# Layer 0 and layer 3 of an adjacency GNN on one Trainium2 core: edge scores by maximum and minimum over sorted columns, and neighbour sums made in the first stage

## The chip, the core and the metric

The kernel runs on one core of one Trainium2 chip. A core has a matrix engine (TensorE, PE in the profile), a vector engine (VectorE, DVE), an activation engine (ScalarE, ACT), GpSimd (POOL) and SyncE (SP). Each works through its own instruction queue in order, and an instruction that waits holds everything behind it in its queue. SP, ACT and POOL also issue DMA transfers from their queues; 16 DMA engines carry them. The metric is the device time of one launch in microseconds; the kernel before takes 3124.82 us, the median of three runs (3122.06 to 3131.15).

## The reference, cut to what matters

```python
# x: (32, 512, 256) f32; adj: (512, 512) f32, symmetric pattern, 4386 non-zero entries
def gnn(h, A, W1, b1, W2, b2, Wa, ba, Wm, bm, beta1, beta2, beta3):      # layers 0 and 3
    pre_u = einsum('bud,dk->buk', h, W1[:256])
    pre_v = einsum('bvd,dk->bvk', h, W1[256:])
    hidden = relu(pre_u[:, :, None, :] + pre_v[:, None, :, :] + b1)
    S = sigmoid(einsum('buvk,ko->buvo', hidden, W2)[..., 0] + b2[0])
    a = einsum('buv,bud->bvd', S * A, h)
    m = einsum('uv,bud->bvd', A, h) * h
    return beta1 * h + beta2 * (a @ Wa + ba) + beta3 * (m @ Wm + bm)
x = gnn(x, adj, L0)                        # layer 0
x = x + relu((adj @ x) @ W.T + b)          # layer 1
f = x @ W1_2.T; f1 = f @ W2_2 + b2_2       # layer 2
c = softmax(leaky_relu(f1[i] + f1[j]) + adj)
x = c @ f + bias2 + x
return gnn(x, adj, L3)                     # layer 3
```

S is needed only where the adjacency has an entry, so it is computed per edge: for an edge (u, v) one takes row u of pre_u + b1, row v of pre_v, and needs the sum over 256 columns k of W2[k] * relu(pu[k] + pv[k]).

## The kernel before, in words

**Two paths.** A short prelude (`Counts`) counts entries per row of the adjacency and writes a number `excess`; if it is positive a dense path runs, else the sparse path. With the given inputs the sparse path runs, and only it is described.

**Groups.** The 32 batches are worked in 8 groups of 4 (`NB`). For each group and each of layers 0 and 3 there is a `Group` with a table in DRAM (1024 rows of 4 x 256 values: for every node its pre_u + b1 row and its pre_v row, for the four batches side by side), a matrix of scores in DRAM (`cells`, two halves), and small tiles on chip (`s`, `self_s`).

**Edges as items.** `Edges.build` turns the adjacency into 36 items of 128 edges each: 8 for every chunk of 128 nodes (`OWN`), of which partition p holds the first to eighth neighbour of node p, and 4 panels for the nodes with more neighbours. To do this it computes ranks, writes four `lists` to DRAM, and for the panels gathers four rows `got` of these lists by index (L368), each needing `inode`, computed last (L345 to L362). Entries on the diagonal are not items.

**The five kinds of streams** of a group, all Python generators:

- `first`: loads h, turns it over on PE (L556), stores hT to DRAM (`xT`, L768), and in `pre` multiplies by W1 (L570, L572). From each PSUM result `pre` makes `puv` on DVE and ACT (L574, L575), the score of the diagonal in two more DVE operations (L577, L578), and writes `puv` to the table on SP's queue (L582).
- `edges`: for each item, fetch the other end's rows from the table by index on POOL's queue (L607) into one of 5 buffers, some items ahead; the own end's rows (`mine`) once per chunk on SP's queue (L647). DVE adds the two, 128x1024 (L686). Then relu, times W2, and the sum over 256 columns for each batch: for every second item in one DVE operation of 128x1024 (L694) and four ACT accumulations (L672), for the others in four accumulating DVE operations of 128x256 (L702). Scores are finished every four items (exp on ACT, L592; L596, L597, L636 on DVE) and scattered into `cells` by index on POOL's queue (L601). Two calls, the very first and the very last, have `spare` buffers, a longer lead, and send every item by L694 and ACT.
- `middle`: loads the score matrix SA (L727, on POOL's queue), and per batch runs layer 0's rest, layers 1 and 2, and `pre` of layer 3. Layer 0's rest needs hWa and the neighbour sums mhT (`mhT`, PE L45 `adj,h` and DVE L750), made at the start of each batch, then zT (L848 on DVE), on which the next PE step L861 waits.
- `last`: layer 3's rest (hWa, mhT, L1001, L1010), out to DRAM. In the last group it is split into `last_before` and `last_behind`.
- `setup` streams: `Edges.build`, scaled weights, and zeroing of `cells` (L538, on SP's queue).

The call for group 0 is special: its hWa and mhT are made ahead (`middle_before`).

**What sets the order.** `sparse_path` gives each piece of each stream a due time in units of a group, and `weave` emits pieces by due time; pieces of kind "fill" (`first`, `last`) are held back and put where the middle stage says that it has room. `behind` adds order constraints that keep edge work behind the middle stage. A tile framework then adds semaphores and orders each engine's queue. PE's queue is thus fixed at build time.

Of the kernel before, what the change touches and what calls it, by code (L numbers as in the profile page):

```python
# [36 lines left out]
SPARE = NC // 2 * OWN * P + LINES  # L37
GROUP = NB * D
HELD = 8
# [8 lines left out]
class Model:  # L48


    def __init__(self, ctx, tc, a):
        nc = self.nc = tc.nc
        self.tc, self.a = tc, a
        const = self.const = ctx.enter_context(tc.tile_pool(name="const", bufs=1))
        self.ident = const.tile([P, P], F32, name="ident")
        make_identity(nc, self.ident)
        self.adj = const.tile([P, NC, N], F32, name="adj")
        for c in range(NC):
            nc.sync.dma_start(self.adj[:, c, :], a["adj"][c * P : (c + 1) * P, :])
        self.g0, self.g3 = self.gnn_first("L0_gnn"), self.gnn_first("L3_gnn")  # L60
# [36 lines left out]
    def gnn_first(self, L):  # L97
# [3 lines left out]
        w["b1bc"] = self.bcast(f"{L}_b1", D)  # L101
        w["W2bc"] = const.tile([P, D], F32, name=f"{L}_W2bc")
        nc.scalar.dma_start(w["W2bc"], a[f"{L}_W2"].rearrange("k o -> (k o)").partition_broadcast(P))
# [7 lines left out]
        return w  # L111

# [63 lines left out]
class Counts:  # L176
# [3 lines left out]
    def __init__(self, ctx, m):  # L180
# [4 lines left out]
        with tc.tile_pool(name="c_sb", bufs=2) as sb, tc.tile_pool(name="c_ps", bufs=1, space=PSUM) as ps:  # L185
# [17 lines left out]
            pc = ps.tile([1, NC], F32, name="pc")  # L203
            nc.tensor.matmul(pc, ones[:, 0:1], self.lines, start=True, stop=True)
            half = sb.tile([1, 2], F32, name="half")
            nc.vector.tensor_reduce(half, pc.rearrange("p (h c) -> p h c", h=2), AX.X, ALU.add)
            most = sb.tile([1, 1], F32, name="most")
            nc.vector.tensor_reduce(most, half, AX.X, ALU.max)
            nc.vector.tensor_scalar(self.excess, most, float(-LINES), None, ALU.add)
# [10 lines left out]
class Edges:  # L220
# [3 lines left out]
    def __init__(self, m, pool):  # L224
# [4 lines left out]
        self.value = pool.tile([P, ITEMS], F32, name="value")  # L229
        self.inode = pool.tile([P, 2 * PANELS], I32, name="inode")  # L230

        order = [item_of(0, j) for j in range(OWN // 2)]
        for lead, other in ((0, 2), (2, 1), (1, 3)):
            for j in range(OWN // 2):
                order += [item_of(lead, OWN // 2 + j), item_of(other, j)]
# [6 lines left out]
    def value_of(self, j):  # L242
        k = self.order.index(j)
        return self.value[:, k : k + 1]

# [3 lines left out]
    def build(self, counts, adjT, lists, psum, big, tmp):  # L249
# [66 lines left out]
        for c in (0, 2, 1, 3):  # L316
            at = slice(c, c + 1)
# [24 lines left out]
            self.slots(js, v, there, t, row[:, at], spare)  # L342
            yield

        js = slice(NC * OWN, ITEMS)  # L345
        pu = psum()[:, 0 : 2 * PANELS]
        ones_bf = bf2[:, 1024:1025]
        nc.vector.memset(ones_bf, 1.0)
        for k in range(2 * PANELS):
            h, q = divmod(k, PANELS)  # L350
            mm(nc, pu[:, k : k + 1], [(full[:, h * 2 + c, q * P : (q + 1) * P], ones_bf) for c in range(2)])
        u, node, slot, start, sp, v, there, t = (sheet(2 * PANELS) for _ in range(8))
        nc.vector.tensor_scalar(u, pu, float(HALF - 1), None, ALU.min)
        nc.vector.tensor_copy(node, u)
        nc.vector.tensor_scalar(node[:, PANELS:], u[:, PANELS:], float(HALF), None, ALU.add)
        inode = self.inode
        nc.vector.tensor_copy(inode, node)
        nc.vector.tensor_scalar(self.iu, node, 2.0, None, ALU.mult)
        nc.gpsimd.iota(slot, [[0, 2], [P, PANELS]], 0, 1, allow_small_or_imprecise_dtypes=True)
        nc.vector.tensor_scalar(start, u, float(N), None, ALU.mult)  # L360
        nc.vector.tensor_scalar(sp, slot, float(CELLS + NC // 2 * OWN * P), None, ALU.add)
        nc.vector.tensor_scalar(t, slot, 1.0, None, ALU.add)  # L362
        yield
        gots = []
        for k in range(2 * PANELS):
            gots.append(tmp.tile([P, 2 * N], F32, name=f"got{k}", tag=("h1", "hT1", "mhT0", "hWa0")[k]))
            index = bass.IndirectOffsetOnAxis(ap=inode[:, k : k + 1], axis=0)
            nc.gpsimd.indirect_dma_start(out=gots[k], out_offset=None, in_=lists, in_offset=index)  # L368
        yield
        for k in range(2 * PANELS):  # L370
# [4 lines left out]
                junk, rank, t[:, at], adj, ALU.is_equal, ALU.mult, accum_out=self.value_of(NC * OWN + k)  # L375
            )
            nc.vector.scalar_tensor_tensor(junk, rank, slot[:, at], ones, ALU.is_le, ALU.mult, accum_out=v[:, at])
            yield
        self.slots(js, v, there, t, start, sp, 0)
# [19 lines left out]
class Group:  # L399

    def __init__(self, sp, w, name):
# [3 lines left out]
        self.s = sp.grp.tile([P, ITEMS, NB], F32, name=f"s{name[0]}")  # L407
        self.self_s = sp.grp.tile([P, NC, NB], F32, name=f"self_s{name[0]}")
# [6 lines left out]
class Sparse:  # L415
# [3 lines left out]
    def __init__(self, ctx, m, counts, xr, outr, B):  # L419
# [12 lines left out]
        self.xT, self.x2T = (self.dram.tile([B, P, DC, N], F32, name=n) for n in ("xT", "x2T"))  # L432
        self.e = Edges(m, pool("edges", 1))
# [76 lines left out]
    def setup(self):  # L510
# [6 lines left out]

        edges = self.built = self.e.build(self.counts, self.adjT, self.lists, self.psum, self.big, self.act)
# [11 lines left out]
    def zeros_behind(self):  # L530
        self.zeros(self.cells["3"])
        yield

    def zeros(self, cells):
        for c in cells:
            flat = c[0:CELLS, :].rearrange("(q p a) b -> q p (a b)", q=4, p=P)
            for q in range(4):
                self.nc.sync.dma_start(flat[q], self.zero)  # L538
# [5 lines left out]
    def setup_rest(self):  # L544
        yield from self.rest
# [14 lines left out]
    def pre(self, g, b, hT):  # L560
# [3 lines left out]
        for c in range(NC):  # L564
# [9 lines left out]
            nc.vector.tensor_tensor(puv[:, 0, :], pp[:, 0:D], w["b1bc"], ALU.add)  # L574
# [788 lines left out]
```

## Time and profile before

| what | value |
|---|---|
| median of three runs | 3124.82 us |
| profiled execution, its own time | 3102.14 us |
| its span, first to last instruction | 3100.4 us |
| mean granted TensorE clock in it | 0.941 |
| PE busy | 2714.6 us (88%) |
| DVE busy | 2302.8 us (74%) |
| POOL busy | 1522.5 us (49%) |
| ACT busy | 1337.8 us (43%) |
| DMA bytes, mean rate | 679.40 MB, 219 GB/s |

How to read what follows: a group line names source line, engine, operation, tile written and tile read, shapes, a count, then busy time and mean duration of one; after the second bar comes the idle time of the engine just before these instructions and what ended it. A line of a waits view says which instruction waited for which, the total, how often, and the longest. A windows line gives a stretch in us from the span's start, its length, the busy time of each engine in it, the granted clock, the busy share of the DMA engines and the rate. fp32 matrix products appear as two passes each, and the counts are of passes.

### The profile page before, as it was taken

How to read it: one execution, taken by the hardware profiler on the slowest of the kernel's cores; microseconds unless marked ns; L12 is line 12 of the kernel's file. 1: busy time of each engine (PE TensorE's matmuls, PEld its weight loads, DVE VectorE, ACT ScalarE, POOL GpSimd, SP SyncE). 2: the span in 40 equal slices, each digit the busy share in tenths (PEclk: the TensorE clock that was granted, in tenths of full speed). 3: DMA queues.
4: the chain of work that ended last, by engine and by line, in shares of the span. 5: the costliest groups of instructions: out<-in, count | busy, mean ns of one | idle time of the engine just before them, and what ended most of it. 6: DMA issues, size and time to landing. Idle time of an engine off the chain costs nothing.

```text
span 3100.4 us, 32465 instructions
## 1 busy us (share of the span) xinstructions
PE 2714.6 (88%) x8645; PEld 1642.5 (53%) x8646; DVE 2302.8 (74%) x6026; ACT 1337.8 (43%) x4101; POOL 1522.5 (49%) x1312
## 2 busy tenths in 40 slices
PE   6366888889998999989998999989999899889957
PEld 3133444446654565546664565545664566545636
DVE  6783886889589875989589885888679795772761
ACT  3453554445345433545354442545335343453440
POOL 1462453556346563556346562565436563450561
PEclk9688988999999999999999999999999999999978
DMA  8874556786677766786668766787568766551753
GB/s 285 282 236 152 180 174 225 237 268 213 223 224 263 235 210 219 247 282 213 227 213 258 238 197 213 242 267 237 188 216 268 251 221 208 178 174 58 234 195 115
DMA packets 302719, 679.40 MB, mean 219 GB/s; under 512 B 52672, under 2 KB 170944, under 8 KB 294336
## 3 DMA queue, kind: packets, MB, share of 16 engines
q0 software_dynamic: 120384, 406.01, 41.0%
q1 hardware_dynamic: 163184, 234.01, 22.5%
q10 hardware_dynamic: 18960, 37.24, 3.2%
q8 instruction: 70, 1.15, 0.2%
q14 instruction: 121, 0.99, 0.1%
HBM read 531.12 MB, written 146.01 MB: 218 GB/s over the span
## 4 chain that ended last, share of the span: by engine, by line
PE 51%; DVE 18%; DMA 17%; issue 6%; ACT 4%; POOL 3%; SPq 0%; POOLq 0%; ACTq 0%; DVEq 0%
PE pst L45 24%; PE pst L1001 7%; DVE rows L686 6%; DMA table<-puv 5%; DMA rows<-table,iv 5%; PE pst L570 3%; DVE rows L702 3%; PE pst L861 3%; PE pst L1010 3%; PE pst L572 3%; DMA cells<-s,cell 3%; DVE rows L694 3%; PE pst L883 2%; PE pst L840 2%; DMA SA<-cells 2%
## 5 line engine op out<-in xcount | busy, mean ns | idle before, releaser
L601 POOL DMA_INDIRECT cells<-s,cell x576 | 691.1, 1200 | 740.7 <-DMA cells<-s,cell 370.3
L607 POOL DMA_INDIRECT rows<-table,iv x554 | 663.3, 1197 | 672.7 <-DMA table<-puv 148.1
L686 DVE TENSOR_TENSOR rows<-rows,mine 128x1024 f32<-128x1024 f32 x554 | 670.8, 1219 | 164.7 <-DMA rows<-table,iv 148.8
L672 ACT ACTIVATE rows<-rows 128x256 f32<-128x256 f32 x1096 | 442.9, 407 | 516.7 <-DVE rows L694 511.1
L45 PE MATMUL pst<-adj,h 128*128 128x512 f32 x1024 | 451.3, 592 | 0.3 <-PE pst L941 0.3
L702 DVE SCALAR_TENSOR_TENSOR rows<-rows,L_gnn_W2bc 128x256 f32<-128x256 f32 x1120 | 415.9, 419 | 1.8
L45 PE MATMUL pst<-L_gnn_Wa,hT 128*128 128x256 f32 x1024 | 264.3, 410 | 118.6 <-DMA hT<-xT 64.6
L694 DVE SCALAR_TENSOR_TENSOR rows<-rows,L_gnn_W2bc 128x1024 f32<-128x1024 f32 x274 | 332.3, 1216 | 0.3
L45 PEld LDWEIGHTS pst<-adj,h 128*128 128x128 f32 x1024 | 192.8, 190 | 222.4 <-issue 218.4
L45 PEld LDWEIGHTS pst<-L_gnn_Wa,hT 128*128 128x128 f32 x1024 | 207.7, 208 | 165.8 <-issue 53.1
L45 PE MATMUL pst<-eT,feats 128*128 128x512 f32 x512 | 231.5, 606 | 12.4 <-ACT eT L953 12.4
L45 PE MATMUL pst<-adjT,zW 128*128 128x512 f32 x512 | 227.8, 597 | 6.2 <-ACT zW L865 6.2
L1001 PEld LDWEIGHTS pst<-hWa,SA 128*128 128x128 f32 x896 | 213.7, 328 | 7.7 <-issue 4.5
L1001 PE MATMUL pst<-hWa,SA 128*128 128x256 f32 x896 | 216.8, 398 | 0.0
L861 PE MATMUL pst<-WT,hT 128*128 128x256 f32 x512 | 150.3, 459 | 75.9 <-DVE hT L848 75.9
L672 ACT ACTIVATION_READ_ACCUMULATOR rows<-rows 128x1 f32 x1096 | 206.7, 189 | 0.0
L809 ACT COPY flat<-SA 128x512 f32<-128x512 f32 x128 | 137.6, 1128 | 155.0 <-PE pst L45 60.1
L840 PE MATMUL pst<-flat,hWa 128*128 128x512 f32 x448 | 196.8, 592 | 0.0
L861 PEld LDWEIGHTS pst<-WT,hT 128*128 128x128 f32 x512 | 118.0, 235 | 114.9 <-DVE hT L848 88.1
L575 ACT COPY puv<-pst 128x256 f32<-128x256 f32 x256 | 93.7, 370 | 183.8 <-DVE puv L574 168.1
L574 DVE TENSOR_TENSOR puv<-pst,bc_L_gnn_b 128x256 f32<-128x256 f32 x256 | 105.0, 416 | 90.3 <-DMA table<-puv 53.8
L45 PEld LDWEIGHTS pst<-eT,feats 128*128 128x128 f32 x512 | 97.5, 193 | 127.5 <-issue 109.8
(170 smaller groups left out, 3979.3 us busy)
## 6 DMA issues: line engine op xcount, KB each, us to landing
table<-puv SPq DMA_DIRECT2D x256, 256.0 KB, 5.5
SA<-cells POOLq DMA_DIRECT2D x64, 1024.0 KB, 7.0
h<-in_x_dram SPq DMA_DIRECT2D x64, 512.0 KB, 6.4
mine<-table SPq DMA_DIRECT2D x64, 512.0 KB, 5.3
hT<-xT SPq DMA_DIRECT2D x36, 512.0 KB, 5.1
h<-x2s SPq DMA_DIRECT2D x36, 512.0 KB, 4.1
xT<-hT ACTq DMA_DIRECT2D x32, 512.0 KB, 5.5
x2T<-yT SPq DMA_DIRECT2D x32, 512.0 KB, 5.3
```

Of the source, the lines that this page charges most:

```text
L45: nc.tensor.matmul(out, lhsT, rhs, start=(n == 0), stop=(n == len(pairs) - 1))
L574: nc.vector.tensor_tensor(puv[:, 0, :], pp[:, 0:D], w["b1bc"], ALU.add)
L601: self.nc.gpsimd.indirect_dma_start(out=g.cells[half], out_offset=bass.IndirectOffsetOnAxis(ap=at, axis=0), in_=s, in_offset=None)
L607: self.nc.gpsimd.indirect_dma_start(out=rows, out_offset=None, in_=g.table, in_offset=bass.IndirectOffsetOnAxis(ap=at, axis=0))
L672: self.behind(nc.scalar.activation(part, part, AF.Identity, accum_out=g.s[:, k, b : b + 1]))
L686: self.behind(nc.vector.tensor_tensor(rows, rows, other, ALU.add))
L694: nc.vector.scalar_tensor_tensor(by_entry, by_entry, 0.0, w2, ALU.max, ALU.mult)
L702: nc.vector.scalar_tensor_tensor(part, part, 0.0, w["W2bc"], ALU.max, ALU.mult, accum_out=at)
L809: self.nc.scalar.copy(flat[:, r, :], SA[r][:, :, b])
L840: nc.tensor.matmul(pz, hWa[:, r, cs], flat[:, r, :], start=(r == 0), stop=False)
L861: nc.tensor.matmul(pw[:, at], zT[:, d, cs], m.WT_1[:, d, :], start=(d + k == 0), stop=(d * k == 1))
L1001: nc.tensor.matmul(pz[:, k * D : (k + 1) * D], SA[r][:, cs, b], hWa[:, r, :], start=(r + k == 0), stop=False)
```

## The change

**Sorted columns.** The columns of W1 are permuted so that columns with positive W2 stand first, scaled by -W2 or W2, and the score of an edge becomes a sum over columns of a maximum (positive W2) or a minimum (negative W2) of two table rows, less a number per node (`less`) that is added up while `puv` is made. In a band of 32 columns around the middle (`MIXED`), where the sign can differ between inputs, a multiplication by `sign` turns one into the other. `sorted` does the permutation at run time with small matrix products, once per layer. An item now takes three DVE operations, of 4x144, 4x32 and 4x112 columns, in place of the addition, and then either four ACT accumulations or one DVE reduction; the multiplication by W2 is gone. ACT takes every second item (two of three in the calls with `spare`).

**Diagonal as turns.** The four chunks of diagonal entries become four more turns of the edge loop (40, `TURNS`), with rows fetched on SP's queue and scores stored on SP's queue; `pre` makes no diagonal score any more. The `less` numbers go through DRAM (16 stores on SP) and 4 small gathers per call on POOL's queue for the panels.

**Neighbour sums with the first layer.** For groups 1 to 7 mhT of layer 0 is made in `first` from the h that is loaded there, stored to DRAM (`mhTs`, SP) and loaded in `middle`, which no longer loads h. `first` of group 2 moves from due time 0.67..0.93 to 0.1..0.45.

**Lists sooner, zeros later.** The gathers of `got` stand before the items of the third chunk. Zeroing moves to POOL's queue; that of layer 3's `cells` waits behind the middle stage.

```diff
+TURNS = ITEMS + NC
+MIXED = slice(D // 2 - 16, D // 2 + 16)
+    def sorted(self, w, t, psum):
...
+        mm(nc, pr[:, 0:1], [(before, positive[:, 0:1])])
+        mm(nc, pr[:, 1:2], [(before, positive[:, 1:2]), (ones, positive[:, 0:1])])
+        mm(nc, pr[:, 2:3], [(ones, positive[:, c : c + 1]) for c in range(DC)])
...
+            nc.vector.tensor_scalar(place[:, c, :], row, to[:, c : c + 1], None, ALU.is_equal)
...
+                nc.tensor.transpose(pt[:, r * P : (r + 1) * P], w["W1"][:, r, c * P : (c + 1) * P], self.ident)
+            nc.scalar.copy(W1T[:, c, :], pt)
...
+        nc.vector.tensor_copy(vs, pw[:, 0:D])
...
+            nc.vector.tensor_tensor(w["W1"][:, r : r + 2, :], by_two(ps), by, ALU.mult)
...
# Counts
+            nc.vector.tensor_scalar(positive, m.cols[:, :, 0, :, 0], 0.0, None, ALU.is_gt)
...
# Edges
+        order = [item_of(0, j) for j in range(OWN // 2)] + [ITEMS]
...
+            order.append(ITEMS + other)
...
# setup
+        self.m.sorted(self.m.g0, self.big(F32, 2048), self.psum)
     def zeros_behind(self):
+        self.behind(self.nc.vector.memset(self.zero, 0.0))
         self.zeros(self.cells["3"])
...
-                self.nc.sync.dma_start(flat[q], self.zero)
+                self.nc.gpsimd.dma_start(flat[q], self.zero)
     def setup_rest(self):
+        self.m.sorted(self.m.g3, self.big(F32, 2048), self.psum)
# pre
-            nc.vector.tensor_tensor(puv[:, 0, :], pp[:, 0:D], w["b1bc"], ALU.add)
+            nc.vector.scalar_tensor_tensor(
+                puv[:, 0, :], pp[:, 0:D], 1.0, w["bu"], ALU.mult, ALU.add, accum_out=part
+            )
             nc.scalar.copy(puv[:, 1, :], pp[:, D:])
-            both = self.small.tile([P, D], F32, name="both", bufs=1)
-            nc.vector.tensor_tensor(both, pp[:, D:], puv[:, 0, :], ALU.add)
             nc.vector.scalar_tensor_tensor(
-                both, both, 0.0, w["W2bc"], ALU.max, ALU.mult, accum_out=g.self_s[:, c, b : b + 1]
+                junk, puv[:, 0, MIXED], 1.0, w["sign"][:, 0, :], ALU.mult, ALU.mult, accum_out=mixed
             )
# edges
+        def less(ks):
...
+                self.behind(nc.vector.tensor_tensor(s, s, by, ALU.subtract))
...
+                    nc.sync.dma_start(diagonal, g.s[:, k, :])
...
-            self.fetch(rows, g, e.iv[:, j : j + 1])
+            if j < ITEMS:
+                self.fetch(rows, g, e.iv[:, j : j + 1])
+            else:
+                nc.sync.dma_start(rows, places[c, 1])
...
-            self.behind(nc.vector.tensor_tensor(rows, rows, other, ALU.add))
+            self.behind(nc.vector.tensor_tensor(rows[:, :, first], rows[:, :, first], other[:, :, first], ALU.max))
+            nc.vector.tensor_tensor(rows[:, :, mixed], rows[:, :, mixed], sign, ALU.mult)
+            self.behind(nc.vector.tensor_tensor(rows[:, :, behind], rows[:, :, behind], other[:, :, behind], ALU.min))
...
+            if k == TURNS // 2:
+                for q in range(2 * PANELS):
+                    nc.gpsimd.indirect_dma_start(
+                        out=g.less[:, NC + q, :], out_offset=None, in_=g.less_dram, in_offset=index
+                    )
...
-            if spare or k % 2 == 1 and k < ITEMS - 3:
-                nc.vector.scalar_tensor_tensor(by_entry, by_entry, 0.0, w2, ALU.max, ALU.mult)
+            if k % 3 < 2 if spare else k % 2 == 1 and k < TURNS - 3:
                 summed.append(lambda k=k, rows=rows: sums(k, rows))
...
-                for b in range(NB):
-                    nc.vector.scalar_tensor_tensor(part, part, 0.0, w["W2bc"], ALU.max, ALU.mult, accum_out=at)
+                nc.vector.tensor_reduce(g.s[:, k, :], rows, AX.X, ALU.add)
# first
+            if i > 0:
+                for mhT in self.mhT(h, hT, 3):
+                    yield
+                self.nc.sync.dma_start(self.mhTs[i + b], mhT)
             yield from self.pre(g, b, hT)
# fresh, middle_one
-            h = self.act.tile([P, NC, D], F32, name="h1")
-            self.nc.sync.dma_start(h, self.xr[i])
+            mhT = self.act.tile([P, DC, N], F32, name="mhT1", tag="h1")
+            self.nc.sync.dma_start(mhT, self.mhTs[i])
...
-        else:
-            for mhT in self.mhT(h, hT, 0):
-                yield
# sparse_path
-            first = spread(FIRST, start - 0.86, start - 0.6)
+            first = spread(FIRST, 0.1, 0.45) if t == 2 else spread(FIRST, start - 0.86, start - 0.6)
...
-            (sp.edges(g0, ("yT", "mhT3") if t == 0 else ()), edges0, ""),
+            (sp.edges(g0, ("yT", "mhT0", "hWa0") if t == 0 else ()), edges0, ""),
```

## The prediction

> **What bounds the kernel now.** I read the windows first, cut at the points where groups change, since a mean hides stages (columns: stretch; its length; busy PE, PEld, DVE, ACT, POOL; granted clock; DMA share; GB/s).
>
> ```profile
> 0.00:85.00 85.00, 57.30 (x177) 30.99 (x178) 58.15 (x212) 33.86 (x87) 16.35 (x29) 0.92 0.84 288
> 85.00:262.00 177.00, 81.09 (x218) 44.49 (x218) 117.88 (x227) 80.56 (x341) 102.30 (x86) 0.75 0.74 256
> 262.00:474.00 212.00, 170.48 (x491) 91.78 (x492) 150.67 (x402) 103.35 (x276) 85.97 (x76) 0.87 0.48 151
> 474.00:711.00 237.00, 206.52 (x610) 112.13 (x609) 191.16 (x526) 106.85 (x324) 123.71 (x106) 0.94 0.77 250
> 711.00:1059.00 348.00, 329.60 (x1074) 200.29 (x1073) 281.79 (x764) 155.26 (x464) 187.29 (x160) 0.98 0.72 236
> 1411.00:1763.00 352.00, 332.40 (x1071) 201.60 (x1069) 281.89 (x764) 155.65 (x464) 187.07 (x162) 0.97 0.73 235
> 2479.00:2880.00 401.00, 376.50 (x1229) 230.50 (x1228) 259.84 (x687) 164.97 (x439) 159.30 (x137) 0.97 0.51 166
> 2880.00:3028.00 148.00, 102.83 (x342) 72.86 (x340) 104.67 (x138) 69.78 (x313) 93.47 (x73) 0.86 0.67 222
> ```
>
> Five like periods, 711 to 2479, take 348 to 359 us each with PE busy 330 to 335 (95%), DVE 282 (80%). PE bounds them; their idle PE sums to 107 us. Before them PE is idle 41.5 + 30.5 us (262 to 711), after them 24.5: 203.7 us in 262 to 2880. The first 262 us (one group's first edges) and the 148 from 2880 (the last edges) are bound by the edge chain.
>
> Next, what PE waits for between 262 and 2880, and what DVE waits for in 85 to 262 and over the whole span (columns: total, times, longest):
>
> ```profile
> PE pst L861 <- DVE hT L848: 75.9, 21, 8.5
> PE pst L952 <- DVE cols L912: 37.6, 6, 8.7
> PE pst L952 <- DVE ex L913: 30.6, 21, 3.3
> ...
> DVE big L374 <- DMA got<-lists,inode: 16.0, 1, 16.0
> ...
> DVE puv L574 <- DMA table<-puv: 53.8, 24, 4.5
> ```
>
> The first three, 144 of PE's 204, are middle-stage results that stand on DVE behind edge work. The fourth is a hole in the opening stage, the fifth counts under the rivals. Last, the groups that the change edits (count, busy, mean ns):
>
> ```profile
> L686 DVE TENSOR_TENSOR rows<-rows,mine 128x1024 f32<-128x1024 f32 x554 | 670.8, 1219 | 164.7 <-DMA rows<-table,iv 148.8 <-DMA mine<-table,iu 13.2 <-issue 1.7
> L672 ACT ACTIVATE rows<-rows 128x256 f32<-128x256 f32 x1096 | 442.9, 407 | 516.7 <-DVE rows L694 511.1 <-ACT x L943 3.2 <-ACT puv L575 1.1
> L702 DVE SCALAR_TENSOR_TENSOR rows<-rows,L_gnn_W2bc 128x256 f32<-128x256 f32 x1120 | 415.9, 419 | 1.8
> L694 DVE SCALAR_TENSOR_TENSOR rows<-rows,L_gnn_W2bc 128x1024 f32<-128x1024 f32 x274 | 332.3, 1216 | 0.3
> ```
>
> The timeline of DVE gives the pitch, since neighbours overlap by about .084 us: two additions take 2.36, a 1024-column operation 1.135, a 256-column accumulating one about .345 (starts at 929.51 and 929.85).
>
> ```profile
> 927.24 2.36 DVE L686 TENSOR_TENSOR rows<-rows,mine 128x1024 f32<-128x1024 f32 x2
> 929.51 0.42 DVE L702 SCALAR_TENSOR_TENSOR rows<-rows,L_gnn_W2bc 128x256 f32<-128x256 f32 x1
> ```
>
> **DVE per item.** Before: an item for ACT costs 2 x 1.135 = 2.27 us, an item for DVE 1.135 + 4 x .345 = 2.515. After: the additions of 1024 (1.219), 512 (.684) and 256 columns (.419) lie on .149 + 1.045 ns per column, which gives .751 for the maximum (576), .283 for the multiplication (128), .617 for the minimum (448): 1.651 less 3 x .084 = 1.40. A DVE turn adds one reduction of 128x1024. None is in the trace; bounds are .75 (a third below an elementwise pass, faster than any f32 row here of two inputs) and 2.0 (four accumulating passes of 256 with their reads, .419 + .081 each). I take an elementwise pass, 1.135, since it reads the same columns: 2.535 a turn.
>
> An ordinary call then goes from 16 x 2.27 + 20 x 2.515 = 86.6 to 18 x 1.40 + 22 x 2.535 = 81.0, and with its few score operations (.6 before; subtractions of `less` bring about 2.3) from 87.2 to 83.3: -3.9. `pre` loses two 256-column operations a chunk and gains one of 32 with its read, 1.015 to .455 us, 16 chunks a call: -9.0. Two calls a period: -26 of 282 (9%). A `spare` call goes from 36 x 2.27 = 81.7 to 27 x 1.40 + 13 x 2.535 less overlaps, about 73. Whole kernel: DVE 2303 to about 2100.
>
> The Trainium skill, VectorE: DVE Perf Modes, section Rules for kernel authors, speaks against this part: operation count is what to minimize, and three replace one here. In the rows four 256-column operations cost 1.38 where one of 1024 costs 1.135, .08 for each added one, so the count matters little at this size. By the rule with no overlap a turn would be 1.65, +160 us of DVE over 640 turns, and two thirds of the DVE gain would go.
>
> **ACT, POOL, DMA, SP.** ACT accumulates .407 + .189 a piece, 2.38 a turn: +4.8 us an ordinary call (ACT is at 44%, hidden). POOL: 4 gathers of `less` a call at 1.2 + .3 issue, +6 on about 94; hidden at 53%. DMA: own-end rows 33.6 MB and mhTs stores 14.7 MB against 679, +7%, share .72 to about .77; hidden unless it delays `table` writes. SP gains 64 row fetches, 32 more diagonal stores, 28 mhTs stores and 16 `less` stores, about 140 entries, each able to wait; what stands behind them is the `puv` store (L582), whose lateness DVE pays at L574. I cost them at nothing: SP's entries are waiting for their producers anyway; uncovered they are rival C.
>
> **PE.** mhT of a group is 4 x 16 passes of 512 columns at .4295 (16 in 6.87 us), 27.5 us. Groups 2 to 7 only move it to `first`: total unchanged. Group 1's goes into the first 262 us, where PE is busy 138 of 262: -27.5 in the span after, full gain if that idle takes it (bounds -27.5, 0 if its products hold up `pre`, whose rows the edges want). Sorting adds 7 us of PE per layer; layer 0's is ahead of all, layer 3's lies within edges of group 0: 0 each beyond the term below.
>
> **Opening, 0 to 262: -12 (bounds -35, +15).** The 16.0 us hole goes, as `got` is asked for some turns ahead. About 16 list scans of .67 us (+10.7) now stand ahead of the first row addition, not after. Layer 3's zeros, 4.2 MB, leave a stretch with DMA at .84 and 288 GB/s: 15 us of transfers, half taken as exposed, -8. `spare` DVE work falls by 8.5 but the chain is mostly latency: -4. The sorting chain stands ahead of the first W1 product; the first table write came only at 38.1 us, behind the zeros, so I count +5 of its estimated 17. Sum -12. Here the Trainium skill (DMA: Bandwidth & Descriptors, section Issuing engines are not separate DMA queues) says that another issuing engine saves only issue time; by it the zeros of layer 0 give nothing, and only the delay of layer 3's would, some -8.
>
> **Idle PE in 262 to 2880: -92 of 203.7 (bounds 0, -204).** In 262 to 711 there are 72 us idle, because there is no filler: `first` of group 2, due at 0.67, now comes from 0.1 and carries 31.7 + 27.5 = 59 us of PE. I take half, 35: the rest is chains within one batch (softmax), and group 1's edges must still be scheduled with DVE. In the five periods, 107 us: the queue on DVE ahead of L848, L912 and L913 shrinks; DVE goes from 80% to 73%, or with a period of 338 to 76%. Waiting behind a backlog falls faster than load; 40% gives 43, 8.6 a period, 353 to about 344. What is late next is PE itself, whose floor is 329.5. In 2479 to 2880, 14 of 24.5, as mhT of the last group no longer stands at the head of its batches. mhT in `middle` is now a load, issued early on SP; if it comes late, PE waits at L847 in place of running it.
>
> **Tail, 2880 to the end: +3 (bounds -8, +15).** Four more turns of latency-bound edges at about 4 us an item, two thirds covered by the cheaper ones, and `less` gathers on POOL, which there is busy 93 of 148.
>
> **Sum**, against the profiled execution, 3102.1: -27.5 - 12 - 35 - 43 - 14 + 3 = -128.5, so 2974. The median of the runs stands at 3124.82 / 3102.14 = 1.0073 of it: 2995.
>
> **Rivals.** A: as forecast, 2995 (own range 2930 to 3050). B: waits are latency in the chains, not DVE load, and only the moved mhT, the opening and the tail count: -36.5, 3066 profiled, 3088. For it: 21 waits at L861 are near 3.6 us each, three DVE operations deep, and shorter operations shorten them little; against it: L686 operations of 2.36 stand directly ahead of them. C, slower: the SP queue holds up the `puv` stores. Each hit costs DVE and then PE 2.24 us (53.8/24). With 140 new entries the gain of 128.5 is gone from .92 us an entry; half of them at 2.24 would be 157, net +28, 3153. For it: SP already stands 484.7 us in front of `puv` stores. Against: these waits are for producers, and only 24 of 256 were felt. D: the reduction costs far more than 2.0; DVE becomes the bound at 344 us a period: 256 + 44 x (t - 1.135) = 344 at t = 3.1 us. At 2.0, DVE is 294, above 282: no gain from backlog, B. E: nearly all the idle goes, mhT and sorted load together, -190: 2912 profiled, 2933. F: the change does not do what it says, if excess were positive and the dense path ran; the trace shows sparse items in all groups, and the test stays, so under .01.
>
> **Chances.** A .55, B .17, C .11 (incl. a larger opening loss), D .03 (half slower), E .13, F .01. Range 2910 to 3095: E, A and B inside, C and D out. Faster than before by over 0.3% (about what a measurement can tell here): A, B, E and half of D, .87; slower .11; same .02.
>
> **What would show it.** DVE busy near 2100; groups of 640 at .75, .28 and .62 us, 334 reductions at 1.2; `adj,h` products before 262; no wait on `got`; L848's wait under half of 75.9; periods of 338 to 346. Wrong: a reduction near 2, a grown wait at L574 for the table, or an opening over 265 us.

## The result and the profile after

The changed kernel takes 3208.57 us (median of four runs) against 3125.64 for the kernel before: a ratio of 1.0263, 95% interval 1.0238 to 1.0288. It is slower by 2.6%, where 2995 was forecast. The profiled execution has a span of 3212.1 us, 111.7 more than before's 3100.4. The medians differ by only 82.9 us: before's profiled execution (3102.14) lies 0.7% under its median and the changed kernel's (3213.80) 0.2% above, so differences read off the two profiles are some 29 us too large in all.

The page's line of busy times of the changed kernel:

```profile
PE 2753.3 (86%) x8729; PEld 1667.2 (52%) x8730; DVE 2109.8 (66%) x5600; ACT 1337.7 (42%) x4185; POOL 1482.3 (46%) x1406
```

Its groups by form, for the work that was priced (count, busy and mean ns; behind the second bar the idle time before, and what ended it):

```profile
L815 DVE TENSOR_TENSOR rows<-rows,mine 128x576 f32<-128x576 f32 x610 | 458.2, 751 | 356.6 <-DMA rows<-table,iv 348.9 <-issue 7.7
L833 DVE TENSOR_REDUCE s<-rows 128x4 f32<-128x1024 f32 x324 | 392.3, 1211 | 2.8
L817 DVE TENSOR_TENSOR rows<-rows,mine 128x448 f32<-128x448 f32 x610 | 375.8, 616 | 0.0
L816 DVE TENSOR_TENSOR rows<-rows,L_gnn_sign 128x128 f32<-128x128 f32 x610 | 169.4, 278 | 0.0
```

Every price of an instruction was right to within 2%: .751, .278, .616 and 1.211 us against .751, .283, .617 and 1.219 forecast, DVE 2109.8 against "about 2100". DVE lost 193 us of work, and the profiled execution became 112 us longer. What grew is in the first line of the groups: the maximum waited 356.6 us for its rows, where before's addition waited 164.7.

The windows of the changed kernel, cut where the zT addition of a group's first batch starts (columns as in the prediction):

```profile
0.00:279.00 279.00, 181.87 (x559) 102.55 (x561) 164.00 (x580) 104.92 (x363) 124.08 (x146) 0.88 0.77 257
279.00:543.00 264.00, 239.29 (x707) 125.73 (x705) 162.11 (x452) 120.61 (x326) 90.95 (x92) 0.95 0.64 209
543.00:887.00 344.00, 270.73 (x840) 167.33 (x840) 240.41 (x594) 149.28 (x470) 178.04 (x164) 0.89 0.68 220
887.00:1259.00 372.00, 338.31 (x1072) 204.69 (x1072) 257.04 (x673) 159.09 (x496) 187.13 (x168) 0.95 0.72 238
1259.00:1635.00 376.00, 335.70 (x1072) 202.42 (x1072) 257.75 (x673) 159.50 (x496) 183.11 (x168) 0.95 0.71 236
1635.00:2006.00 371.00, 334.14 (x1072) 201.99 (x1072) 258.18 (x674) 159.43 (x496) 183.89 (x168) 0.95 0.73 239
2006.00:2372.00 366.00, 333.22 (x1072) 201.81 (x1072) 257.10 (x673) 159.74 (x496) 181.25 (x168) 0.96 0.72 242
2372.00:2734.00 362.00, 331.54 (x1053) 199.64 (x1054) 255.71 (x669) 159.09 (x496) 179.00 (x167) 0.96 0.73 237
```

Cut at the same events, before has 277.5 for the opening, 231.1, 344.4, and then 350.0, 350.8, 355.8, 358.3, 350.9. So the opening gave +1.1, middle 0 +33.8, the stage after it -0.9, the five periods +81.4 and the rest (481.7 to 477.9) -3.8: 111.6 together. The loss sits in the periods, where DVE fell from 282 to 257 us, and PE's idle rose from 107 to 174 us; the other 14 of the 81 us are PE's own work, which took longer (last section).

PE's longest waits in the changed kernel (total, times, longest):

```profile
PE pst L995 <- DVE hT L982: 72.0, 23, 9.0
PE pst L49 <- DMA hT<-x2T: 51.5, 5, 20.2
PE pst L49 <- ACT puv L682: 48.7, 7, 11.5
```

DVE's, of which before had 148.8 and 53.8:

```profile
DVE rows L815 <- DMA rows<-table,iv: 348.9, 108, 17.3
DVE puv L679 <- DMA table<-puv: 97.5, 34, 5.3
```

PE's first line answers to before's wait at L861 (75.9): all but unmoved, with a lighter DVE. Its third is new, seven times: PE waits for ACT to evict a result of `pre` (copy it out of PSUM, where PE has put it). The timeline of POOL around one such place (start, duration, in brackets the idle time before) shows what leads to it:

```profile
1590.18 0.99 POOL L707 DMA_INDIRECT cells<-s,cell  x1 [2.50 <-DMA cells<-s,cell]
1594.68 0.97 POOL L707 DMA_INDIRECT cells<-s,cell  x1 [3.51 <-DMA cells<-s,cell]
1605.35 1.13 POOL L859 DMA_DIRECT2D SA<-cells  x2 [1.46 <-DMA cells<-s,cell]
1623.61 1.00 POOL L713 DMA_INDIRECT rows<-table,iv  x1 [17.12 <-DMA table<-puv]
```

and so does that of ACT:

```profile
1610.89 1.09 ACT L946 COPY flat<-SA 128x512 f32<-128x512 f32 x1 [13.66 <-DMA SA<-cells]
1611.88 0.64 ACT L682 COPY puv<-pst 128x256 f32<-128x256 f32 x2
```

The last edge turn of this call was at 1585.0. Six scatters (L707) followed it, most of them held until an earlier one had landed; the last started at 1602.9, and only then did POOL load the rest of the score matrix (1605). ACT's copy of it stood idle 13.7 us, with `pre`'s evictions queued behind it, whose products PE had finished by 1602.7. On the evictions hangs the table, on the table the next call's first rows (1623.6). In before three or four scatters follow the last turn of such a call, in the changed kernel five to eight.

This makes a circuit: edge turns, scatters, score load, middle stage, table, edge turns. A period holds one edge call of layer 3 and one of layer 0. Cut at the starts of their first and last turns, it falls into four parts, which sum to it by construction: the table says where the time lies, not yet what sets it ("step" is from the layer-3 call's last turn to the layer-0 call's first; read off the timelines, means over four groups, us):

| kernel | layer-3 call | step | layer-0 call | gap to the next call | sum |
|---|---|---|---|---|---|
| before | 149.6 | 6.7 | 153.5 | 44.2 | 354.0 |
| changed | 161.0 | 3.7 | 159.0 | 47.8 | 371.5 |

Of the 17.5 us by which the period grew, the two calls hold 16.9 and the gap 3.6, less 3.0 in the step. So the late evictions belong to the smaller part of the loss. A turn did not get slower (149.6 us over 35 intervals is 4.3, 161.0 over 39 is 4.1); there are more of them.

### The profile page after: what moved, and what is told of

It is laid out like the page before. It is cut to its first block, busy times and chain, and to the rows that moved or that the text cites. A ratio compares the mean times of both kernels' runs of the same rounds, so it can differ in the third digit from the quotient of the medians.

```text
span 3212.1 us, 32792 instructions
## 1 busy us (share of the span) xinstructions
PE 2753.3 (86%) x8729; PEld 1667.2 (52%) x8730; DVE 2109.8 (66%) x5600; ACT 1337.7 (42%) x4185; POOL 1482.3 (46%) x1406
## 5 line engine op out<-in xcount | busy, mean ns | idle before, releaser
L707 POOL DMA_INDIRECT cells<-s,cell x576 | 649.6, 1128 | 909.1 <-DMA cells<-s,cell 459.8
L713 POOL DMA_INDIRECT rows<-table,iv x552 | 597.6, 1083 | 574.0 <-DMA table<-puv 202.8
L799 ACT ACTIVATE rows<-rows 128x256 f32<-128x256 f32 x1144 | 462.4, 406 | 691.3 <-DVE rows L817 335.6
L815 DVE TENSOR_TENSOR rows<-rows,mine 128x576 f32<-128x576 f32 x610 | 458.2, 751 | 356.6 <-DMA rows<-table,iv 348.9
L49 PE MATMUL pst<-L_gnn_Wa,hT 128*128 128x256 f32 x1024 | 276.5, 423 | 145.8 <-DMA hT<-x2T 51.5
L833 DVE TENSOR_REDUCE s<-rows 128x4 f32<-128x1024 f32 x324 | 392.3, 1211 | 2.8
L817 DVE TENSOR_TENSOR rows<-rows,mine 128x448 f32<-128x448 f32 x610 | 375.8, 616 | 0.0
L49 PEld LDWEIGHTS pst<-L_gnn_Wa,hT 128*128 128x128 f32 x1024 | 216.5, 216 | 195.1 <-issue 76.0
L49 PE MATMUL pst<-eT,feats 128*128 128x512 f32 x512 | 252.5, 651 | 33.3 <-ACT eT L1087 33.1
L679 DVE SCALAR_TENSOR_TENSOR puv<-pst,L_gnn_bu 128x256 f32<-128x256 f32 x256 | 106.4, 418 | 247.1 <-DMA table<-puv 97.5
L49 PE MATMUL pst<-adjT,zW 128*128 128x512 f32 x512 | 227.8, 596 | 3.9 <-ACT zW L999 3.9
L946 ACT COPY flat<-SA 128x512 f32<-128x512 f32 x128 | 137.7, 1126 | 176.2 <-DMA SA<-cells 104.0
```

Source lines behind the costliest of these rows:

```text
L49: nc.tensor.matmul(out, lhsT, rhs, start=(n == 0), stop=(n == len(pairs) - 1))
L679: nc.vector.scalar_tensor_tensor(puv[:, 0, :], pp[:, 0:D], 1.0, w["bu"], ALU.mult, ALU.add, accum_out=part)
L707: self.nc.gpsimd.indirect_dma_start(out=g.cells[half], out_offset=bass.IndirectOffsetOnAxis(ap=at, axis=0), in_=s, in_offset=None)
L713: self.nc.gpsimd.indirect_dma_start(out=rows, out_offset=None, in_=g.table, in_offset=bass.IndirectOffsetOnAxis(ap=at, axis=0))
L799: self.behind(nc.scalar.activation(part, part, AF.Identity, accum_out=g.s[:, k, b : b + 1]))
L815: self.behind(nc.vector.tensor_tensor(rows[:, :, first], rows[:, :, first], other[:, :, first], ALU.max))
```

## The experiments

Ratios are to the kernel before, run beside each on the same chip; 1% is 31 us. The chips differ between runs, and before's own median was 3112.5 to 3129.1 us beside them, so times in us, and the expectations in us, carry that play. Two pictures stood against each other at first: the loop of edge calls sets the period (EDGES), or the neighbour sums, taken from the head of each batch, bring PE too early to a zT addition that waits behind an edge turn (HEAD).

**a_nodiag: no diagonal turns.**

```diff
-TURNS = ITEMS + NC
+TURNS = ITEMS
-        order = [item_of(0, j) for j in range(OWN // 2)] + [ITEMS]
+        order = [item_of(0, j) for j in range(OWN // 2)]
-            order.append(ITEMS + other)
```

> The changed kernel with the four diagonal turns of each edge call left out (36 turns, no own-row fetches, no diagonal stores; the scores of diagonal entries are left out of the result). Theory EDGES: the loop of edge calls sets the period (two calls of 161 us and a gap of 48 are the 372 us that a period takes), and eight turns of 4.0 us go out of each period at half their length or more: periods of 350 to 358, 3090 to 3130 us in all. Theory HEAD: what sets the period is that the neighbour sums no longer stand at the head of each batch of the middle stage, so that PE comes to the zT addition early; the turns matter little: 3180 to 3205.

3085.72 us, 0.9877 (0.9830 to 0.9924): 3.9% under the changed kernel, 121 us for 64 turns, just below what EDGES expected. PE's wait for `pre`'s evictions is still there (41.4 us, 7 times, against 48.7), so that wait is not what the turns cost.

**a_mhTmid: the third part undone.**

```diff
-            if i > 0:
-                for mhT in self.mhT(h, hT, 3):
-                    yield
-                self.nc.sync.dma_start(self.mhTs[i + b], mhT)
...
+        else:
+            for mhT in self.mhT(mhT, hT, 0):
+                yield
...
-            first = spread(FIRST, 0.1, 0.45) if t == 2 else spread(FIRST, start - 0.86, start - 0.6)
+            first = spread(FIRST, start - 0.86, start - 0.6)
```

> The changed kernel with its third part undone: mhT is made at the head of each batch of the middle stage again, from h, and first of group 2 has its old due time. Theory EDGES: the calls have 40 turns as before this edit, periods stay at 365 to 375; 3200 to 3240 us, since group 1's mhT is no longer hidden in the opening. Theory HEAD: PE's wait in front of the zT addition and the idle around it goes back to that of before, and the lighter DVE shows: 3050 to 3120.

3233.99, 1.0338 (1.0291 to 1.0385), as EDGES expected. HEAD falls: with mhT back at the head the kernel is slower still. In this kernel the third part is worth some 23 us.

**a_first2late: only the last line of that edit.**

> The changed kernel with first of group 2 at its old due time (0.67 to 0.93) alone. The early one made the middle stage of group 0 33 us longer and left 73 us of idle PE in the next stage of 344 us. EDGES: the next stage was bound by edges anyway, so the work is free in its old place: 3175 to 3195. HEAD: the same PE work stands somewhere in both, within 10 us of 3208.

3202.72, 1.0269 (1.0216 to 1.0323): no difference from 1.0263, as HEAD and not EDGES expected. The early `first` of group 2 is worth nothing here. The two stages trade: without it middle 0 takes 235.1 us and the next stage 360.0, with it 264.9 and 343.5.

**b_mhT2: before, with the third part alone** (the a_mhTmid edit the other way round).

> The kernel before with the third part of the change alone: mhT of groups 1 to 7 made in first and loaded in the middle stage, first of group 2 early. EDGES: edge calls are as in before, so periods stay at 350 to 355 or below, and group 1's mhT leaves: 3070 to 3120. HEAD: the periods lengthen as in the changed kernel, by 15 to 20 us each: 3180 to 3230.

3149.13, 1.0081 (1.0050 to 1.0112): between the two expectations, so neither picture has it. The periods stretch by some 7 us, and the early `first` leaves a stage with 65 us of idle PE.

What is it in a turn that costs? ROWS (its fetch and its place among five buffers) against WORK (its DVE time):

**a_diag_rows and a_diag_nofetch: turns with the fetch and no arithmetic, and the reverse.**

```diff
+            own = e.order[k] >= ITEMS
+            if not own:
...
+            if own:
+                nc.vector.tensor_copy(g.s[:, k, :], rows[:, :, 0])
```

The second puts `mate` in place of `rows` as first operand of the maximum and the minimum:

```diff
+            mate = other if e.order[k] >= ITEMS else rows
...
-            else:
-                nc.sync.dma_start(rows, places[c, 1])
```

> The changed kernel whose diagonal turns keep their place and their fetch of own rows, but do no arithmetic: one copy of 4 values in place of the three operations and the sum (the diagonal scores are left out of the result). Some 140 us of DVE work less over 64 turns. Theory ROWS: a turn costs its place in the rotation of five row buffers with a lead of three, and its transfer: 3180 to 3210 us. Theory WORK: a turn costs its DVE time, since DVE stands in front of the middle stage's results: 3085 to 3110.

> The changed kernel whose diagonal turns do all their arithmetic, but on the rows that are on chip already, without the 512 KB fetch of own rows on SP's queue (the diagonal scores are wrong by that, the work is the same). ROWS: most of the 123 us comes back, 3090 to 3130. WORK: nothing comes back, 3195 to 3210.

3173.10, 1.0165 (1.0094 to 1.0236), and 3156.48, 1.0123 (1.0055 to 1.0190). Of the 121 us, 31 go without the arithmetic and 44 without the fetch, each with some 20 either way; neither run met an expectation of either theory. The two need not add up, and no run keeps the turn without both; if they do add up, some 46 us are left for the turn's place in the loop.

**a_lead4: rows asked for four turns ahead.**

```diff
-LEAD = 3
+LEAD = 4
+            if summed:
+                summed.pop(0)()
             if k + lead < TURNS:
                 fetch(k + lead)
...
-            if summed:
-                summed.pop(0)()
```

> The changed kernel with rows asked for four turns ahead in place of three, in the same five buffers (ACT's sums of a turn are put ahead of the next fetch). ROWS: DVE's 349 us of waits for gathered rows fall by a third or more, 3120 to 3170. WORK: within 15 us of 3208.

3186.98, 1.0221 (1.0155 to 1.0287): 0.4% less, within the intervals, and as neither theory expected. DVE's wait for gathered rows fell only from 348.9 to 326.9 us. A longer lead gives little.

**a_self: 36 turns, the diagonal in `pre`** (a complete version; the a_nodiag edit and this).

```diff
+            nc.vector.tensor_tensor(both[:, 0:e], pp[:, D : D + e], puv[:, 0, 0:e], ALU.max)
+            nc.vector.tensor_tensor(both[:, e:], pp[:, D + e :], puv[:, 0, e:], ALU.min)
+            nc.vector.scalar_tensor_tensor(
+                both, both, 1.0, w["signs"], ALU.mult, ALU.mult, accum_out=g.self_s[:, c, b : b + 1]
+            )
```

> A full version: the changed kernel with 36 turns, the diagonal scores made in pre again, now by a maximum of 144, a minimum of 112 and one accumulating operation of 256 columns (.75 us a chunk in DVE's pitch, 192 us in all, more than the 160 of the turns). ROWS, and any theory in which the turn as such costs: 3085 to 3110, as without the diagonal. WORK: 3200 or above.

3099.09, 0.9931 (0.9897 to 0.9966): WORK falls. The page's busy line of a_nodiag:

```profile
PE 2712.7 (88%) x8729; PEld 1651.3 (53%) x8730; DVE 1977.2 (64%) x5150; ACT 1287.7 (42%) x3897; POOL 1442.6 (47%) x1406
```

and of a_self:

```profile
PE 2722.0 (88%) x8730; PEld 1659.6 (54%) x8730; DVE 2170.1 (70%) x6240; ACT 1292.3 (42%) x3913; POOL 1457.4 (47%) x1408
```

193 us of DVE work in `pre` cost 0.5%, 17 us, and the intervals of the two runs overlap. The 64 turns held 133 us of DVE work (2109.8 to 1977.2) and cost 121. DVE's load has next to no price here; the turns have one.

**a_turns32: four turns fewer again.**

```diff
-TURNS = ITEMS + NC
+TURNS = NC * OWN
-            order += tail[j : j + 1]
-        self.order = order
+        self.order = order + tail
```

> The changed kernel with 32 turns a call: neither the diagonal nor the four panel items (the scores of both are left out of the result). With 36 turns a period took 353 us, with 40 it took 369. Theory EDGES: the loop of edge calls is still the bound at 36 turns, and a period falls by another 14 to 18 us: 335 to 340 us, 2990 to 3020 in all. Theory FLOOR: at 36 turns PE's own work (330 us a period) and the waits within a batch bound it, and DVE or edge work taken off buys nothing: periods of 349 to 354, 3060 to 3085.

2959.48, 0.9466 (0.9446 to 0.9486), another 4.1%, more than EDGES expected: the edge loop binds at 36 turns too, at 2 us of run time a turn. These four turns carry more than those of the diagonal: each has two gathers and a scatter on POOL's queue (POOL's entries in a period fall from 168 to 144 below), so the 2 us are not the price of a turn alone. Windows of a_nodiag, two periods:

```profile
1215.00:1567.00 352.00, 329.87 (x1071) 200.85 (x1072) 240.79 (x617) 153.91 (x462) 174.11 (x168) 0.97 0.74 240
1567.00:1924.00 357.00, 330.36 (x1075) 200.47 (x1073) 241.38 (x618) 153.93 (x462) 175.68 (x168) 0.97 0.72 236
```

of a_turns32:

```profile
1157.00:1493.00 336.00, 324.96 (x1073) 197.87 (x1072) 227.28 (x580) 146.45 (x428) 147.37 (x144) 0.98 0.69 225
1493.00:1830.00 337.00, 326.40 (x1072) 198.74 (x1072) 226.84 (x579) 146.34 (x428) 148.60 (x144) 0.98 0.70 226
```

At 36 turns a_nodiag's period is 352 to 357 with DVE at 241, and it was 350 to 358 in before with DVE at 282: 41 us of DVE work less, nothing gained.

**a_self_mid, b_mhT, a_self_lead4: the third part and the lead again, at 36 turns** (the edits are those above; b_mhT is b_mhT2 without the early `first`).

> The full version with 36 turns and the diagonal in pre (3099 us), with the third part undone: mhT at the head of each batch of the middle stage, first of group 2 at its old time. The third part was worth -25 us in the changed kernel and +25 on the kernel before. Theory LOAD: it pays where DVE is light, since PE then finds the zT addition done sooner: 3120 to 3140. Theory TURNS: it pays only where 40 turns hold the edge loop, and costs at 36: 3065 to 3085.

> The kernel before with mhT made in first, but with first of group 2 at its old due time; with the early one it took 3149 us. If the early time is what costs (a hole of 65 us idle PE in the stage after it): 3100 to 3125. If it is the move of mhT out of the head of each batch: 3140 to 3155.

> The full version with 36 turns and rows asked for four turns ahead. EDGES: as with 40 turns, 15 to 25 us less than 3099. FLOOR: rows are no longer what the period waits for, 3090 to 3105.

3131.09, 1.0007 (0.9978 to 1.0037): the third part is worth 0.8% with the new edge work, the size that LOAD expected; LOAD's reason was not tested. This run is also the nearest to the sorted columns alone: DVE is busy 2172.8 us in it, 130 less than in before, and the time is that of before. 3124.48, 0.9985 (0.9970 to 0.9999): alone on the kernel before the third part is worth nearly nothing, and the early `first` costs it 30 us. 3111.12, 0.9925 (0.9898 to 0.9952): the lead does nothing at 36 turns.

What holds the rows? Four runs on POOL's queue:

**a_noless and a_lessbeh: the small gathers of `less` left out, or ordered later.**

```diff
-            if k == TURNS // 2:
-                for q in range(2 * PANELS):
...
+            cs = [c if c < NC else 0 for c in cs]
```

and the order:

```diff
-                    nc.gpsimd.indirect_dma_start(
+                    self.behind(nc.gpsimd.indirect_dma_start(
```

> The changed kernel without the four small gathers of less per call on POOL's queue (the panels subtract chunk 0's numbers, so their scores are wrong; the work is the same). In POOL's queue the four stand right behind the fifth row gather of a call and hold the sixth up by some 5.8 us. Theory SUPPLY: rows that come late from POOL's queue are what took the gain of the lighter DVE: 3150 to 3180. Theory TURNS ALONE: only the number of turns counts: 3195 to 3210.

> The changed kernel, complete, with the four gathers ordered behind the middle stage's work as the edge arithmetic is, so that they stand some ten POOL entries later in the call. SUPPLY: half of what leaving them out gives or more, 3165 to 3195. TURNS ALONE: 3195 to 3210.

3181.57, 1.0233 (1.0186 to 1.0279), and 3229.38, 1.0372 (1.0351 to 1.0393). Leaving them out gives 0.3%, not clear of the intervals; ordering them later costs 1.1%; neither theory expected either. That they hold up the sixth row gather can be seen in the trace, but weighs little in the time.

**a_halfput: half of the scatters left out.**

```diff
-                self.put(g, *r)
+                if r[0] == 0:
+                    self.put(g, *r)
```

> The changed kernel with only half of the score scatters: those into the second half of cells are left out (18 fewer entries a call on POOL's queue, each 1.13 us and a wait for the one before it to land; the scores of half the nodes are left out of the result). SUPPLY, with POOL's queue as what holds the rows: 3100 to 3160. If rows wait for transfers or for free buffers and not for POOL's queue: 3190 to 3210.

3023.89, 0.9708 (0.9691 to 0.9726): 5.5%, 173 us, at the same 40 turns, fetches and DVE work, and more than SUPPLY expected. DVE's wait for gathered rows fell from 348.9 to 229.1 us. Windows of a_halfput, two periods, DVE as heavy as in the changed kernel and PE idle 12 to 15 us:

```profile
1191.00:1532.00 341.00, 328.67 (x1072) 199.25 (x1072) 257.30 (x673) 159.76 (x496) 143.24 (x132) 0.98 0.75 258
1532.00:1875.00 343.00, 328.14 (x1074) 198.66 (x1072) 258.26 (x674) 159.48 (x496) 142.07 (x132) 0.98 0.76 259
```

ACT's wait for the score matrix, 104.0 us (17 times) in the changed kernel, is in a_halfput:

```profile
ACT flat L947 <- DMA SA<-cells: 8.5, 4, 3.6
```

The circuit again, with the runs that moved it:

| kernel | layer-3 call | step | layer-0 call | gap | sum |
|---|---|---|---|---|---|
| a_nodiag | 150.7 | 7.6 | 151.7 | 43.9 | 353.9 |
| a_turns32 | 149.6 | 4.8 | 145.8 | 36.4 | 336.6 |
| a_halfput | 158.0 | 3.7 | 147.5 | 34.7 | 343.9 |

Against the changed kernel, halving the scatters shortens the gap by 13.1, the layer-0 call by 11.5 and the layer-3 call by 3 us. The scatters left out are just those on which the later half of the score load waits, and in all periods none is left behind a layer-0 call's last turn; so the run shortens POOL's queue and frees the score load at once.

**a_self_lessbeh: the order of a_lessbeh on a_self.**

> The full version with 36 turns, the diagonal in pre, and the four gathers ordered behind the middle stage. SUPPLY: 10 to 40 us below 3099. TURNS ALONE: 3090 to 3105.

3102.60, 0.9960 (0.9946 to 0.9975): no gain, as TURNS ALONE expected.

**a_flat and a_self_flat: ACT's copies of the scores ordered behind the last evictions of the stage before.**

```diff
+            self.ended = nc.scalar.copy(x2, by_two(pt)).ins.name
...
+            if b == 0 and self.ended:
+                self.tc.add_manual_dep(copied.ins, self.ended, order, reason="behind the stage before")
```

> The changed kernel, complete, with one order added on ACT's queue: the four copies of the next group's scores (flat) stand behind the last evictions of the stage before. In the changed kernel the third flat copy waits up to 16 us for the score matrix, and pre's evictions, whose products were done some 9 us earlier, wait behind it; on them hang the table, the first rows of the next edge call and so the period. Theory CIRCUIT (edges, scatters, score load, ACT, table, edges): 6 to 9 us a period leave, 3135 to 3175. Theory EDGES ONLY (the turns themselves bound, the gap between calls is hidden): 3195 to 3215.

> The full version with 36 turns and the diagonal in pre (ratio 0.993), with the same order on ACT's queue. CIRCUIT: 25 to 60 us below it, 3040 to 3075. EDGES ONLY: 3090 to 3110.

3192.87, 1.0241 (1.0193 to 1.0290): nearly nothing, where CIRCUIT expected 3135 to 3175. 3073.63, 0.9873 (0.9826 to 0.9921), within what CIRCUIT expected and the best complete version: 1.3% under the kernel before, 3.8% under the changed one, and 0.6% under a_self, with intervals that overlap. PE's waits in a_flat show what took the place of the old wait:

```profile
PE pst L978 <- ACT flat L947: 66.4, 14, 13.2
PE pst L999 <- DVE hT L986: 66.0, 19, 8.4
```

The wait for evictions (48.7 us) is gone, the gap to the next call fell from 47.8 to 39, but the layer-3 call grew from 161.0 to 166.7, and PE now waits for the copied scores themselves (66.4). With 40 turns the score matrix is late whatever the order. In a_self_flat, with 36 turns and three or four scatters after the last, PE's wait for the copied scores is 25.8 us; that this gives the 0.6% is likely, not shown.

## Why the prediction was wrong, by its own steps

**The prices of instructions** held, as shown above, and so did DVE's total. The rule on operation counts that the prediction weighed did not bite: the three operations cost what their rows said and overlap as forecast, 1.41 us from the start of the first (1584.95) to that of what followed them (1586.36). Two slips in the working did not matter: 27 x 1.40 + 13 x 2.535 is 70.8 and not about 73, and 160 of some 203 us is four fifths and not two thirds.

**"Waiting behind a backlog falls faster than load; 40% gives 43" is the step that failed**, with the 35 and 14 that rest on the same thought. It took PE's waits on DVE results (L861, L952) for a matter of DVE's load. In before's trace that was half the story: of the 21 waits at L861, six (36 of 76 us) come behind an edge addition whose rows were late, the others behind edge work that ran without a break. In the changed kernel 22 of 23 (71 of 72 us) come behind a turn whose rows were late, as here, where the zT addition (L982) stands behind such a turn:

```profile
1632.46 0.76 DVE L815 TENSOR_TENSOR rows<-rows,mine 128x576 f32<-128x576 f32 x1 [16.78 <-DMA rows<-table,iv]
1635.13 0.68 DVE L982 TENSOR_TENSOR hT<-hT,pst 128x512 f32<-128x512 f32 x1
```

A lighter turn waits longer for its rows: 348.9 us in all against 148.8. At 36 turns the period was the same at 282 and at 241 us of DVE; 193 us of DVE work added in `pre` cost 17. The five periods gave +81 between the two profiles where -43 was forecast.

**The diagonal turns were priced as DVE work inside a call, and their fetches and stores at nothing.** Four turns more lengthen both calls of a period and leave five to eight scatters after the last one. They cost 121 us. Without them (a_nodiag) the change would have gained 38 us of the 128.5 forecast. The sum had no term for a turn as such, because the prediction had put the edges off the path in the periods and bound them only in the opening and the tail.

**mhT of group 1 into the opening, -27.5:** the opening took it (PE busy 147 to 181 us up to the first zT addition, +1.1 us), and the whole third part is worth about 23 us in the changed kernel, give or take 17. The size was near here, but this does not show that the forecast's reason was right: on the kernel before, with the same move into the opening, it is worth 5.

**`first` of group 2 early, -35:** zero. The work filled middle 0 (PE idle 38.0 to 25.2) and made it 33.8 us longer; the stage after it kept its length of 344 with 73 us of idle PE in place of 28. a_first2late shows the trade within the changed kernel: the early `first` takes 16.5 us off the later stage and puts 29.8 onto middle 0. Why middle 0 grows by more than the idle time it fills was not tested.

**Opening -12:** +1.1. The hole at `got` shrank from 16.0 to 7.0 us and the first call's last addition came 2.7 us earlier (230.5 to 227.8), but the first row addition moved from 90.0 to 98.0. What the zeros and the sorting chain took of this no run separates. **Tail +3:** the last call took 124.6 us against 122.9.

**Rivals.** C had the sign but not the mechanism. DVE's wait for `table` stores grew from 53.8 to 97.5 us, but in runs that are 1.4%, 3.9% and 5.5% faster than the changed kernel it stays at 103.1 (a_diag_nofetch), 83.8 (a_nodiag) and 103.5 (a_halfput), so its growth is not what costs. B (latency, not load) was right about the periods and still missed that the edge calls would grow.

**What stays open.** Scatters may act by making the score matrix late (the gap) or by holding row gathers in POOL's queue (the calls); a_halfput changes both, and the calls' 14.5 us are not separated from the gap's 13.1 beyond the table. Whether the 44 us of the own rows' fetch are the transfer or its place in SP's queue was not tried. Nor is it shown what holds a turn to 4.1 to 4.3 us, with less DVE work as with more.

## What to carry to other kernels

Before pricing a lighter engine, ask whether its idle time ends on data: an engine that is 80% busy and waits for gathered rows may give nothing back when its arithmetic shrinks, and a row wait that grows by what the work lost is the sign. Where two streams hand results to each other, cut the period at the starts and ends of the calls (here two edge calls, with scatters, score load and table between them) and see which part grew. The parts always sum to the period, so only a run that shortens one of them shows that it counts, and a part that shrinks can come back in another, as in a_flat. Extra items of a loop can cost their place in it, and the same arithmetic put into another stage can be nearly free: 193 us of DVE work for 17 us.

## What the runs showed of the hardware

- A reduction of 128x1024 to 128x4 on DVE takes 1.211 us, as long as an elementwise pass over the same columns (1.216 to 1.219 in before).
- Where PE idled more, the same work took it longer. The 1072 passes of a period took 329.7, 329.0, 333.0 and 334.1 us in before (granted clock 0.98 to 0.97, 20 to 24 us idle), 338.3, 335.7, 334.1 and 333.2 in the changed kernel (0.95 to 0.96, 33 to 40 us idle), and 325 to 327 in a_turns32 (0.98, 11 us idle). The sum had no term for this; it is 3.9 us a period on average between before and the changed kernel, with ranges that touch.
- Scatters by index cost time although POOL is busy for only 46% of the span: 288 of 576 left out took 301 us off POOL's busy time (1482.3 to 1180.9) and 173 off the kernel.
